# Expert biases moved from TensorE's matmuls to VectorE's additions, with merged tokens padded to 32 columns

## The chip, the cores and the metric

The kernel runs on one core of a Trainium2 chip. The metric is the device time of one execution in microseconds (us); of several executions the median is given. A core has five engines that work through their own queues: TensorE (matmuls and transposes, into PSUM), VectorE (DVE in the profile), ScalarE (ACT), GpSimd (POOL) and SyncE (SP), whose queue issues most of the DMAs. Everything here is computed in 32-bit floats, apart from a few small mask and bias operands in bf16.

## The reference, cut to what matters

Two transformer layers act on x of shape 8 x 512 x 256 (batch elements, tokens, channels). The first layer adds attention (16 heads of 64) and a mixture of 32 experts to x; the second adds a small associative memory and a feed-forward net with routed blocks. The change touches the experts of the first layer alone:

```python
logits = einsum('bsd,ed->bse', x, gate_w) + gate_b
probs = softmax(logits, axis=-2)                 # over the tokens
vals, idx = top_k(probs, 8)                      # each expert picks 8 tokens of each batch element
merged = einsum('bked,bke->bed', tok, vals)      # ... and merges them into one
h = einsum('bei,eih->beh', concat([merged, ones]), w1)   # 257 x 1024 an expert
h = gelu(h)
o = einsum('bej,ejo->beo', concat([h, ones]), w2)        # 1025 x 256 an expert
out = scatter-add of o * vals to the chosen tokens
```

So each expert sees eight merged tokens, one for each batch element. The last row of w1 (row 256) and of w2 (row 1024) of each expert is a bias: it is multiplied by one and added.

## The kernel before, in words

The program has three stretches. The first (to about 102 us) loads x, normalises it, transposes it, and computes the gate's logits, the chosen tokens' weights (`psel`) and the merged tokens. A merged token of expert e and batch element b is a column of `mT` (channels on the partitions; `mT` has an index for the channel half `dc`, the expert and the batch element, the last with 8 entries). The matmuls that merge (`pmg`, L373) are done for four batch elements at a time, and L380 copies the result to `mT`.

The second stretch (to about 1290 us) holds the attention, in 32 iterations (8 batch elements of 4 head groups), and the experts. Its order on TensorE, VectorE, ScalarE and GpSimd is written out by a planner (`Plan`, L49): each piece of work is an `op` with an engine, an estimated cost in ns, the pieces that it depends on, a priority in units of attention work, and the buffers (`acq`, `rel`) that it takes and gives back. The planner plays through time and always issues the piece that can start first within a horizon of 12 units. Each engine then works its list strictly in that order. SyncE's order is not among the planner's: the DMAs are put in a row when the program is built, by when what each waits for is expected. The buffers that matter here: `mm` and `tr` are two PSUM banks each, used by projections (`pq`, L456; `pv`, L464), by the output projection (`po`, L786) and by the experts' matmuls on the one hand, and by transposes (`pqk`, L514; `pgt`, L639; `pp`, L723), the attention's value matmuls (`y`, L756) and the experts' transposes on the other; `ew` are the six buffers for expert weights, 512 KB each.

The experts are worked in eight groups of four (`expert`, L845), one group for each batch element of attention, since the work of a group hides in that of the attention. Each of the four experts has a band of 32 PSUM partitions, of which the kernel before uses eight. A group has these steps:

1. Twice (once for each half of the 1024 hidden units): load four weight tiles, one an expert (L821). A bias matmul (L861) writes all 128 partitions of the bank with the experts' biases, from `b1g` (4 x 1024) and the selector `sel` as the stationary operand, and starts the accumulation. Then eight matmuls (L867), one for each expert and channel half, add their 8 x 512 products: the four experts' column bands of the array work side by side. VectorE copies the bank to `eh` (L874).
2. TensorE transposes `eh` (L888) in two sets of four into `tr` banks, and ScalarE applies Gelu from PSUM (L893), reading 8 of each 32 columns, into `ehT`. This gives the `tr` banks back.
3. Twice (once for each half of the hidden units): load four weight tiles (L828). In the first half a bias matmul (L918, from `b2g`) starts the accumulation. Sixteen matmuls (L925) follow. After the first half VectorE copies the bank to `osb` (L934). After the second it adds the bank to `osb` band by band, eight rows at a time (L938), and SyncE sends each band's rows to `o_all` (L940).

In the profile each 32-bit matmul stands as two matmul records, and a transposition as one: L867 has 256 records for its 128 instructions.

The third stretch (from about 1293 us) is the second layer. Its weights are first loaded into six tiles of the pool that held the expert weights (`raw1` twice, `raw2` twice, `raw3`, `raw4`; L980 to L983) and transposed (L1015, L1029, L1040 to L1051); then the batch elements follow each other.

Of the kernel before, what the change touches and what calls it, by code (L numbers as in the profile page):

```python
# [8 lines left out]
F32 = mybir.dt.float32  # L9
BF16 = mybir.dt.bfloat16  # L10
AF = mybir.ActivationFunctionType
ALU = mybir.AluOpType
# [127 lines left out]
def tile_two_layer_block(  # L140
# [31 lines left out]
    ewp = ctx.enter_context(tc.tile_pool(name="ew", bufs=6))  # L172
# [27 lines left out]
    for h in range(2):  # L200
# [22 lines left out]

    sel = const.tile([EPG, EPG, 32], F32, tag="sel", name="sel")
    nc.gpsimd.memset(sel, 0.0)
    nc.gpsimd.affine_select(
        out=sel, in_=sel, compare_op=ALU.not_equal, fill=1.0, base=0,
        pattern=[[-1, EPG], [0, 32]], channel_multiplier=1,
    )
# [62 lines left out]
    mT = const.tile([P, NC, E, B], F32, tag="mT", name="mT")  # L292
# [5 lines left out]
    with tc.tile_pool(name="pa", bufs=2) as pa, tc.tile_pool(name="pa1", bufs=1) as pa1:  # L298
# [86 lines left out]

        for h in range(2):
            nc.scalar.dma_start(w128[h * D : (h + 1) * D, 0:1], q_rms_w.unsqueeze(1))
            nc.scalar.dma_start(w128[h * D : (h + 1) * D, 1:2], k_rms_w.unsqueeze(1))
# [39 lines left out]
    with tc.tile_pool(name="pb", bufs=2) as pb, tc.tile_pool(name="pb1", bufs=1) as pb1:  # L428
# [5 lines left out]
            prT=2, yT=NPR * NHG + 3, xr=1, nm=3, sums=3, rinv=3, ew=6, eh=1, ehT=1, eb=1,  # L434
# [369 lines left out]
        def load_stage(m, w):  # L804
# [3 lines left out]
            def bias():  # L808
                rows = slice(g * EPG, (g + 1) * EPG)
                b1g = pb.tile([EPG, FH], F32, tag="b1g", name=f"b1g_{g}", bufs=1)  # L810
                nc.sync.dma_start(b1g, ew1[rows, C, :])
                b2g = pb.tile([EPG, C], F32, tag="b2g", name=f"b2g_{g}", bufs=1)
                nc.sync.dma_start(b2g, ew2[rows, FH, :])
                ebias[g] = b1g, b2g
# [30 lines left out]
        def expert(g, when):  # L845
# [7 lines left out]
            for half in range(2):  # L853
                ld = load_stage(4 * g + half, when[half] - NU)

                def hidden(half=half):
                    m = 4 * g + half
                    if half == 0:
                        s.h = pb.tile([P, FH], F32, tag="eh", name=f"eh_{g}", bufs=1)
                    s.ph = mm_tile(f"ph_{g}_{half}")  # L860
                    nc.tensor.matmul(  # L861
                        s.ph, sel.rearrange("k q r -> k (q r)"),
                        ebias[g][0][:, half * 512 : (half + 1) * 512], start=True, stop=False,
                    )
                    for dc in range(NC):
                        for q in range(EPG):
                            nc.tensor.matmul(  # L867
                                s.ph[32 * q : 32 * q + B, :], mT[:, dc, g * EPG + q, :],
                                ew[m, q][:, dc * 512 : (dc + 1) * 512],
                                start=False, stop=(dc == NC - 1),  # L870
                            )
# [4 lines left out]
                hd = op("PE", 2800, hidden, ld, when[half], acq=["mm"] + ["eh"] * (half == 0),  # L876
# [3 lines left out]
                def turn(half=half):  # L880
                    if half == 0:
                        s.hT = pb.tile(
                            [P, FH // P, EPG, B], F32, tag="ehT", name=f"ehT_{g}", bufs=1
                        )
# [14 lines left out]
                s.turn, s.gelu = turn, gelu  # L899
                out_ops.append((ho, turn, gelu))  # L900
            acts = []
            for half, (ho, turn, gelu) in enumerate(out_ops):
# [4 lines left out]
            for half, (ho, turn, gelu) in enumerate(out_ops):  # L907
                gl.append(op("ACT", 270 + 1283 * (1 - half), gelu, acts, when[2] + 0.1 + 0.01 * half,
                             rel=["tr"]))
            prev = []  # L910
            for half in range(2):
                ld = load_stage(4 * g + 2 + half, when[3 + half] - NU)

                def down(half=half):
                    m = 4 * g + 2 + half
                    s.po[half] = mm_tile(f"peo_{g}_{half}")
                    if half == 0:
                        nc.tensor.matmul(  # L918
                            s.po[0][:, :C], sel.rearrange("k q r -> k (q r)"), ebias[g][1],
                            start=True, stop=False,  # L920
                        )
                    for c in range(4):
                        for q in range(EPG):
                            k = half * 4 + c
                            nc.tensor.matmul(  # L925
                                s.po[half][32 * q : 32 * q + B, :C], s.hT[:, k, q, :],
                                ew[m, q][:, c * C : (c + 1) * C],
                                start=(half == 1 and c == 0), stop=(c == 3),
                            )

                def o_out(half=half):
                    if half == 0:
                        s.osb = pb.tile([P, C], F32, tag="osb", name=f"osb_{g}", bufs=1)
                        nc.vector.tensor_copy(s.osb, s.po[0][:, :C])  # L934
                        return
                    for q in range(EPG):
                        rows = slice(32 * q, 32 * q + B)
                        nc.vector.tensor_add(s.osb[rows, :], s.osb[rows, :], s.po[1][rows, :C])  # L938
# [310 lines left out]
```

## Time and profile before

| | us |
|---|---|
| Median of 3 runs | 1664.84 (1663.77 to 1667.19) |
| The profiled execution, its own time | 1665.2 |
| Span of the profiled execution | 1663.5 |
| TensorE busy | 1593.1 (96%) |
| VectorE busy | 922.3 (55%) |
| ScalarE busy | 700.5 (42%) |
| GpSimd busy | 590.7 (36%) |
| DMA, mean over the span | 54 GB/s |

A row of the profile names the source line, the engine, the operation, the tile written and the tile read, the shapes and the number of instructions. In rows of the timeline the first two numbers are the start and the length in us, and an entry in brackets is the time for which the engine stood idle before it and what released it. PE is TensorE at its matmuls, and PEld TensorE loading the stationary operand, which can overlap. For a matmul "128*8 128x512" means a stationary operand of 128 rows and 8 columns, and a moving one of 512 columns. Matmuls are pipelined, so the distance between the starts of two rows tells more than the length of one.

### The profile page before, as it was taken

The numbers are of one execution on the slowest core, as the hardware profiler recorded it, in microseconds if no ns is written. First come the engines' busy times: TensorE is split into PE (matmuls) and PEld (weight loads), VectorE is DVE, ScalarE is ACT, GpSimd is POOL, SyncE is SP. The second block draws the span as 40 slices with busy tenths as digits, with TensorE's granted clock in tenths as the row PEclk, the third lists the DMA queues.
The fourth block names the chain that finished last, engine by engine and source line by source line (L and its number), as shares of the span: only waits on it lengthen the run. The fifth ranks groups of instructions, "written<-read, shape, count | busy, mean of one in ns | idle before, by whom it ended". The sixth has DMA issues, their size and how long they took to land.

```text
span 1663.5 us, 26380 instructions
## 1 busy us (share of the span) xinstructions
PE 1593.1 (96%) x9416; PEld 933.3 (56%) x9416; DVE 922.3 (55%) x2682; ACT 700.5 (42%) x1918; POOL 590.7 (36%) x1082
## 2 busy tenths in 40 slices
PE   4789999999999999999999999999999899999999
PEld 1455555655665565565556556655655655555555
DVE  5537666666666665665666676666666332333331
ACT  1115554455446544544555454455545121222221
POOL 4016444444444444534444444444444100000000
PEclk9679999999999999999999999999999899999999
DMA  8000113032011302211130122123014000000000
GB/s 267 26 4 1 52 53 106 8 105 81 30 58 52 103 11 81 77 57 58 52 103 7 58 79 80 46 67 103 7 58 138 14 10 13 14 13 13 13 13 16
DMA packets 72914, 89.26 MB, mean 54 GB/s; under 512 B 5016, under 2 KB 55984, under 8 KB 72784
## 3 DMA queue, kind: packets, MB, share of 16 engines
q1 hardware_dynamic: 71552, 86.87, 16.0%
q8 instruction: 75, 1.23, 0.3%
q10 hardware_dynamic: 1232, 0.71, 0.2%
q14 instruction: 55, 0.45, 0.1%
HBM read 83.11 MB, written 4.19 MB: 52 GB/s over the span
## 4 chain that ended last, share of the span: by engine, by line
PE 89%; DVE 3%; ACT 1%; issue 1%; POOL 0%; ACTq 0%; DVEq 0%; POOLq 0%
PE pq L456 13%; PE sc L688 9%; PE pp L723 9%; PE y L756 9%; PE ph L1179 7%; PE py L1197 7%; PE po L786 7%; PE pv L464 6%; PE pqk L514 4%; PE sc L678 4%; PE peo L925 2%; PE ph L867 2%; PE sc L683 1%; PE ph L1183 1%; PE py L1195 1%; PE ph L861 1%
## 5 line engine op out<-in xcount | busy, mean ns | idle before, releaser
L710 POOL TENSOR_SCALAR pr<-pr,rinv 128x384 f32<-128x384 f32 (+3 forms) x512 | 265.9, 532 | 424.8 <-DVE rinv L707 244.3
L700 ACT ACTIVATE pr<-sc,nm 128x384 f32<-128x384 f32 (+3 forms) x512 | 266.2, 527 | 139.3 <-DVE nm L694 73.9
L241 POOL TENSOR_TENSOR rsqk<-ss,nhalf 128x8 f32<-128x8 f32 x128 | 210.8, 1647 | 146.5 <-DVE ss L491 140.9
L456 PE MATMUL pq<-wqk_sb,xnT 128*128 128x512 f32 x512 | 247.4, 606 | 3.3 <-DVE gl L482 3.3
L694 DVE TENSOR_REDUCE nm<-sc 128x2 f32<-128x768 f32 (+3 forms) x256 | 209.8, 823 | 73.4 <-PE sc L688 70.7
L723 PE MATMUL pp<-ident,pr 128*128 128x128 f32 x1280 | 218.9, 281 | 4.9 <-DVE prT L733 2.7
L723 PEld LDWEIGHTS pp<-ident,pr 128*128 128x128 f32 x1280 | 147.7, 141 | 122.0 <-issue 60.0
L688 PE MATMUL sc<-kT,qT 64*128 64x384 f32 (+3 forms) x1024 | 201.0, 471 | 0.0
L731 ACT COPY prT<-pp 128x384 f32<-128x384 f32 (+3 forms) x256 | 107.2, 426 | 156.4 <-PE pp L723 154.5
L733 DVE COPY prT<-pp 128x384 f32<-128x384 f32 (+3 forms) x256 | 123.4, 487 | 84.2 <-PE pp L723 81.2
L756 PE MATMUL y<-prT,v 128*64 128x256 f32 (+3 forms) x1024 | 152.2, 439 | 0.7 <-ACT prT L731 0.7
L464 PE MATMUL pv<-wvg_sb,xnT 128*128 128x260 f32 x512 | 136.4, 389 | 8.0 <-DVE osb L938 6.8
L456 PEld LDWEIGHTS pq<-wqk_sb,xnT 128*128 128x128 f32 x512 | 87.9, 192 | 85.3 <-issue 70.7
L1179 PE MATMUL ph<-xT,w1T 128*128 128x512 f32 x256 | 128.7, 620 | 0.0
L756 PEld LDWEIGHTS y<-prT,v 128*64 128x64 f32 x1024 | 68.4, 136 | 105.0 <-issue 63.4
L1197 PE MATMUL py<-w2T,hT 128*128 128x256 f32 x512 | 124.0, 388 | 0.0
L786 PE MATMUL po<-wp_sb,yT 128*128 128x256 f32 x512 | 116.4, 381 | 0.0
L1105 POOL TENSOR_TENSOR xres<-x,b_bc 128x1024 f32<-128x1024 f32 x8 | 18.8, 2344 | 265.1 <-DVE x L1098 265.1
L471 ACT ACTIVATE sq<-pq 128x512 f32<-128x512 f32 x128 | 76.3, 596 | 81.4 <-PE pq L456 78.6
L464 PEld LDWEIGHTS pv<-wvg_sb,xnT 128*128 128x128 f32 x512 | 89.0, 191 | 36.8 <-issue 14.6
L1197 PEld LDWEIGHTS py<-w2T,hT 128*128 128x128 f32 x512 | 93.3, 190 | 25.7 <-issue 15.3
L488 DVE TENSOR_REDUCE ss<-sq 128x8 f32<-128x512 f32 x128 | 87.4, 683 | 35.7 <-ACT sq L471 34.9
(187 smaller groups left out, 2067.7 us busy)
## 6 DMA issues: line engine op xcount, KB each, us to landing
ew<-in_L_ffn_w_dram SPq DMA_DIRECT2D x128, 512.0 KB
xt<-in_L_attn_x_dram SPq DMA_DIRECT2D x8, 512.0 KB
xr<-in_L_attn_x_dram SPq DMA_DIRECT2D x32, 128.0 KB
out_dram<-ot SPq DMA_DIRECT2D x32, 128.0 KB
raw<-in_L_ffn_w_dram SPq DMA_DIRECT2D x4, 512.0 KB
wqk_sb<-in_L_attn_Wq_dram SPq DMA_DIRECT2D x2, 512.0 KB
wqk_sb<-in_L_attn_Wk_dram SPq DMA_DIRECT2D x2, 512.0 KB
wvg_sb<-in_L_attn_Wv_dram SPq DMA_DIRECT2D x2, 512.0 KB
```

The source lines that it names most:

```text
L241: nc.gpsimd.tensor_tensor(r, src, nhalf[:, :n], ALU.pow)
L456: nc.tensor.matmul(s.pq[t], xnT[b][:, dc, cols], wqk_sb[:, dc, g, :], start=(dc == 0), stop=(dc == NC - 1),)
L464: nc.tensor.matmul(s.pv[t][:, : GW + HG], xnT[b][:, dc, cols], wvg_sb[:, dc, g, :], start=(dc == 0), stop=(dc == NC - 1),)
L688: nc.tensor.matmul(m.sc[:, h, :w], s.qT[k, q, n0:w], s.kT[k, q, :w], start=False, stop=True)
L694: nc.vector.tensor_reduce(m.nm, m.sc[:, :, :w], AX.X, ALU.max, negate=True)
L700: nc.scalar.activation(m.p[:, h, :], m.sc[:, h, :w], AF.Exp, bias=m.nm[:, h : h + 1], accum_out=m.sums[:, h : h + 1],)
L710: nc.gpsimd.tensor_scalar(m.p[:, h, :], m.p[:, h, :], m.rinv[:, h : h + 1], 1.0, ALU.mult, ALU.mult)
L723: nc.tensor.transpose(m.pt[h][:, d * P : (d + 1) * P], m.p[:, h, j * P : (j + 1) * P], ident)
L756: nc.tensor.matmul(pp.yp[h * D : (h + 1) * D, j * P :], s.v[j][:, hh * D : (hh + 1) * D], pp.tri[:, h, j : j + 4 * (NT - 1 - j) + 1 : 4, : ...
L786: nc.tensor.matmul(o.po[:, :C], yT[b * nk + k][:, t * P : (t + 1) * P], wp_sb[:, k, :], start=(k == 0), stop=(k == nk - 1),)
L1179: nc.tensor.matmul(ph, w1T[:, dc, k * P : (k + 1) * P], s.xT[:, dc, :], start=(dc == 0), stop=False,)
L1197: nc.tensor.matmul(py[:, :C], hT[:, c, cols], w2T[:, c, :], start=False, stop=(c == NFC - 1),)
```

## The change

The bias matmuls are left out. The hidden layer's bias is loaded once in the first stretch (`eb1`, 32 x 1024), transposed by eight small transposes and kept as `eb1T`; VectorE adds it, broadcast over the 32 columns of each expert, when it moves the transposed hidden units from PSUM to `ehT`. Gelu then runs on ScalarE from `ehT` to itself, and the `tr` bank is given back by VectorE's addition. The output's bias is loaded to all 32 partitions of each band by four broadcast DMAs per group, and VectorE adds it where it copied the first half's bank. As no matmul fills the other 24 rows of a band any more, the merged tokens are padded: `mT` gets 32 columns for each expert, cleared once by GpSimd, and the experts' matmuls write all 32 rows of their band. The second half's bank is added by one instruction over 128 rows instead of four over 8. To make room in SBUF the weight buffers go from six to five. The planner's costs are set anew; each expert matmul step is now given 1716 ns.

```diff
-    ewp = ctx.enter_context(tc.tile_pool(name="ew", bufs=6))
+    ewp = ctx.enter_context(tc.tile_pool(name="ew", bufs=5))
...
-    sel = const.tile([EPG, EPG, 32], F32, tag="sel", name="sel")
-    nc.gpsimd.memset(sel, 0.0)
-    nc.gpsimd.affine_select(
...
-    mT = const.tile([P, NC, E, B], F32, tag="mT", name="mT")
+    eb1T = const.tile([P, FH // P, E], F32, tag="eb1T", name="eb1T")
+    mT = const.tile([P, NC, E, 32], F32, tag="mT", name="mT")
+    nc.gpsimd.memset(mT, 0.0)
...
+        eb1 = pa1.tile([E, FH], F32, tag="eb1", name="eb1")
+        nc.sync.dma_start(eb1, ew1[:, C, :])
+        pb1T = tr_tile("pb1T")
+        for k in range(FH // P):
+            nc.tensor.transpose(
+                pb1T[:, k * E : (k + 1) * E], eb1[:, k * P : (k + 1) * P], ident[:E, :E]
+            )
+        nc.vector.tensor_copy(eb1T, pb1T[:, : FH // P * E].rearrange("p (k e) -> p k e", e=E))
...
-            prT=2, yT=NPR * NHG + 3, xr=1, nm=3, sums=3, rinv=3, ew=6, eh=1, ehT=1, eb=1,
+            prT=2, yT=NPR * NHG + 3, xr=1, nm=3, sums=3, rinv=3, ew=5, eh=1, ehT=1, eb=1,
...
-                b1g = pb.tile([EPG, FH], F32, tag="b1g", name=f"b1g_{g}", bufs=1)
-                nc.sync.dma_start(b1g, ew1[rows, C, :])
-                b2g = pb.tile([EPG, C], F32, tag="b2g", name=f"b2g_{g}", bufs=1)
-                nc.sync.dma_start(b2g, ew2[rows, FH, :])
-                ebias[g] = b1g, b2g
+                ebias[g] = pb.tile([P, C], F32, tag="b2g", name=f"b2g_{g}", bufs=1)
+                for q in range(EPG):
+                    nc.sync.dma_start(
+                        ebias[g][32 * q : 32 * (q + 1), :],
+                        ew2[g * EPG + q, FH, :].partition_broadcast(32),
+                    )
...
-                    nc.tensor.matmul(
-                        s.ph, sel.rearrange("k q r -> k (q r)"),
-                        ebias[g][0][:, half * 512 : (half + 1) * 512], start=True, stop=False,
-                    )
                     for dc in range(NC):
                         for q in range(EPG):
                             nc.tensor.matmul(
-                                s.ph[32 * q : 32 * q + B, :], mT[:, dc, g * EPG + q, :],
+                                s.ph[32 * q : 32 * (q + 1), :], mT[:, dc, g * EPG + q, :],
                                 ew[m, q][:, dc * 512 : (dc + 1) * 512],
-                                start=False, stop=(dc == NC - 1),
+                                start=(dc == 0), stop=(dc == NC - 1),
                             )
...
-                hd = op("PE", 2800, hidden, ld, when[half], acq=["mm"] + ["eh"] * (half == 0),
+                hd = op("PE", 1716, hidden, ld, when[half], acq=["mm"] + ["eh"] * (half == 0),
...
-                            [P, FH // P, EPG, B], F32, tag="ehT", name=f"ehT_{g}", bufs=1
+                            [P, FH // P, EPG, 32], F32, tag="ehT", name=f"ehT_{g}", bufs=1
...
                 def gelu(half=half):
-                    nc.scalar.activation(
-                        s.hT[:, half * 4 : (half + 1) * 4],
-                        s.pt[half].rearrange("p (c q r) -> p c q r", c=4, q=EPG)[:, :, :, :B],
-                        AF.Gelu,
-                    )
+                    hT = s.hT[:, half * 4 : (half + 1) * 4]
+                    nc.scalar.activation(hT, hT, AF.Gelu)
+
+                def bias(half=half):
+                    c = slice(half * 4, (half + 1) * 4)
+                    nc.vector.tensor_add(
+                        s.hT[:, c],
+                        s.pt[half].rearrange("p (c q r) -> p c q r", c=4, q=EPG),
+                        eb1T[:, c, g * EPG : (g + 1) * EPG].unsqueeze(3).to_broadcast(
+                            [P, 4, EPG, 32]
+                        ),
+                    )
...
-                acts.append(tn)
+                acts.append(op("DVE", 598, bias, [tn], when[2] + 0.05 + 0.01 * half, rel=["tr"]))
...
-                gl.append(op("ACT", 270 + 1283 * (1 - half), gelu, acts, when[2] + 0.1 + 0.01 * half,
-                             rel=["tr"]))
+                gl.append(op("ACT", 586 + 1283 * (1 - half), gelu, acts, when[2] + 0.1 + 0.01 * half))
...
-                    if half == 0:
-                        nc.tensor.matmul(
-                            s.po[0][:, :C], sel.rearrange("k q r -> k (q r)"), ebias[g][1],
-                            start=True, stop=False,
-                        )
...
-                        nc.vector.tensor_copy(s.osb, s.po[0][:, :C])
+                        nc.vector.tensor_add(s.osb, s.po[0][:, :C], ebias[g])
                         return
+                    nc.vector.tensor_add(s.osb, s.osb, s.po[1][:, :C])
                     for q in range(EPG):
-                        rows = slice(32 * q, 32 * q + B)
-                        nc.vector.tensor_add(s.osb[rows, :], s.osb[rows, :], s.po[1][rows, :C])
...
-                dn = op("PE", 1750 + 350 * (half == 0), down, ld + gl, when[3 + half], acq=["mm"],
+                dn = op("PE", 1716, down, ld + gl, when[3 + half], acq=["mm"],
...
-                prev = [op("DVE", 334 if half == 0 else 1350, o_out, [dn] + prev,
+                prev = [op("DVE", 334, o_out, [dn] + prev,
```

More of the change, by code (lines that the diff above doesn't have):

```diff
@@ L222, in tile_two_layer_block @@
                 )
-    sel = const.tile([EPG, EPG, 32], F32, tag="sel", name="sel")
-    nc.gpsimd.memset(sel, 0.0)
-    nc.gpsimd.affine_select(
-        out=sel, in_=sel, compare_op=ALU.not_equal, fill=1.0, base=0,
-        pattern=[[-1, EPG], [0, 32]], channel_multiplier=1,
-    )
     nhalf = const.tile([P, 64], F32, tag="nhalf", name="nhalf")
@@ L808, in bias @@
             def bias():
-                rows = slice(g * EPG, (g + 1) * EPG)
-                b1g = pb.tile([EPG, FH], F32, tag="b1g", name=f"b1g_{g}", bufs=1)
-                nc.sync.dma_start(b1g, ew1[rows, C, :])
-                b2g = pb.tile([EPG, C], F32, tag="b2g", name=f"b2g_{g}", bufs=1)
-                nc.sync.dma_start(b2g, ew2[rows, FH, :])
-                ebias[g] = b1g, b2g
+                ebias[g] = pb.tile([P, C], F32, tag="b2g", name=f"b2g_{g}", bufs=1)
[4 more added lines that the diff above has]
+                    )
             def weights(q):
@@ L892, in gelu @@
                 def gelu(half=half):
-                    nc.scalar.activation(
-                        s.hT[:, half * 4 : (half + 1) * 4],
-                        s.pt[half].rearrange("p (c q r) -> p c q r", c=4, q=EPG)[:, :, :, :B],
-                        AF.Gelu,
-                    )
-                s.turn, s.gelu = turn, gelu
-                out_ops.append((ho, turn, gelu))
+                    hT = s.hT[:, half * 4 : (half + 1) * 4]
[8 more added lines that the diff above has]
+                        ),
+                    )
+                out_ops.append((ho, turn, bias, gelu))
             acts = []
-            for half, (ho, turn, gelu) in enumerate(out_ops):
+            for half, (ho, turn, bias, gelu) in enumerate(out_ops):
                 tn = op("PE", 436, turn, [out_ops[0][0], out_ops[1][0]], when[2] + 0.01 * half,
                         acq=["tr"] + ["ehT"] * (half == 0), rel=["eh"] * (half == 1))
-                acts.append(tn)
+                acts.append(op("DVE", 598, bias, [tn], when[2] + 0.05 + 0.01 * half, rel=["tr"]))
             gl = []
-            for half, (ho, turn, gelu) in enumerate(out_ops):
-                gl.append(op("ACT", 270 + 1283 * (1 - half), gelu, acts, when[2] + 0.1 + 0.01 * half,
-                             rel=["tr"]))
+            for half, (ho, turn, bias, gelu) in enumerate(out_ops):
+                gl.append(op("ACT", 586 + 1283 * (1 - half), gelu, acts, when[2] + 0.1 + 0.01 * half))
             prev = []
@@ L925, in down @@
                             nc.tensor.matmul(
-                                s.po[half][32 * q : 32 * q + B, :C], s.hT[:, k, q, :],
+                                s.po[half][32 * q : 32 * (q + 1), :C], s.hT[:, k, q, :],
                                 ew[m, q][:, c * C : (c + 1) * C],
-                                start=(half == 1 and c == 0), stop=(c == 3),
+                                start=(c == 0), stop=(c == 3),
                             )
```

## The prediction

> **What bounds the kernel now.** I read the totals by engine and the chain that ended last, then the busy time of each engine by stretch, then TensorE's own rows around the four places that the change touches, then its waits.
>
> The page's totals, and the head of its chain:
>
> ```profile
> PE 1593.1 (96%) x9416; PEld 933.3 (56%) x9416; DVE 922.3 (55%) x2682; ACT 700.5 (42%) x1918; POOL 590.7 (36%) x1082
> ...
> PE 89%; DVE 3%; ACT 1%; issue 1%; POOL 0%; ACTq 0%; DVEq 0%; POOLq 0%
> ```
>
> Busy time by stretch (length, then PE, PEld, DVE, ACT, POOL, granted clock, DMA share, GB/s); the rows of one batch element in mid-run:
>
> ```profile
> 325.00:473.00 148.00, 146.71 (x995) 86.78 (x992) 95.58 (x272) 76.40 (x224) 67.29 (x124) 1.00 0.19 62
> 473.00:621.00 148.00, 145.99 (x980) 86.23 (x979) 94.55 (x266) 75.64 (x223) 67.28 (x124) 1.00 0.19 62
> ```
>
> TensorE is busy 146 of 148 us at the full granted clock; VectorE has a third of its time free, ScalarE half, DMA four fifths. What leaves TensorE's queue there leaves the time, unless another engine then makes it wait.
>
> **Part 1: 24 bias matmuls go.** TensorE's rows around a hidden-layer step and an output step:
>
> ```profile
> 176.95 0.44 PE L723 MATMUL pp<-ident,pr 128*128 128x128 f32 x2
> 177.32 1.12 PE L861 MATMUL ph<-b1g,sel 4*128 4x512 f32 x2
> 178.37 1.90 PE L867 MATMUL ph<-ew,mT 128*8 128x512 f32 x16
> 180.21 0.44 PE L723 MATMUL pp<-ident,pr 128*128 128x128 f32 x2
> ```
>
> ```profile
> 246.13 0.69 PE L918 MATMUL peo<-b2g,sel 4*128 4x256 f32 x2
> 246.76 1.91 PE L925 MATMUL peo<-ew,ehT 128*8 128x256 f32 x32
> 248.60 0.44 PE L723 MATMUL pp<-ident,pr 128*128 128x128 f32 x2
> ```
>
> From start to start L861 holds the queue 178.37 - 177.32 = 1.05 us and L918 0.62 us; the records give 1.051 in all 16 cases and 0.624 in all 8. The change of array tiling that L867 and L925 pay (0.20 us from the row before) is paid today by the bias matmul, and the second L925 of a group, which has no bias ahead of it, pays the same 0.20; so the whole 1.05 and 0.62 go. 16 x 1.051 + 8 x 0.624 = **-21.8 us**.
>
> **Part 2: the stationary operand grows from 8 to 32 columns.** No row has 32. Weight loads (PEld) of the first rounds, of L867 with 8 columns and of L756 with 64:
>
> ```profile
> 178.37 0.12 PEld L867 LDWEIGHTS ph<-ew,mT 128*8 128x8 f32 x8 [0.76 <-issue]
> 178.81 0.11 PEld L867 LDWEIGHTS ph<-ew,mT 128*8 128x8 f32 x4 [0.32 <-issue]
> ...
> 250.75 0.20 PEld L756 LDWEIGHTS y<-prT,v 128*64 128x64 f32 x4 [0.76 <-ACT qT L519]
> 251.23 0.14 PEld L756 LDWEIGHTS y<-prT,v 128*64 128x64 f32 x2 [0.28 <-issue]
> ```
>
> The first round takes 0.44 us with 8 columns and 0.48 with 64; the later rounds of 512 columns take 0.43 in both. So 24 more columns cost some 0.02 us once in each of 32 steps: +0.6 us (0 to 1.5, the latter at 64 columns' price). The Trainium skill speaks against this: "TensorE: Matmul & The Clock Gate" says under "LDWEIGHTS" that a load takes columns / 1.2 ns, so 20 ns more each, and under "Measured speedup vs the span model" that a load overlaps a running matmul only when the row group differs. The four experts' tiles share all rows, so by the page 768 loads would cost +15.4 us in the open. The records show the second round's loads starting 2 ns after a matmul of the same rows has begun (178.802 after 178.800), so they do overlap here; I take **+0.6**, and keep 15.4 only as an outer end. With it the sum below would be -10.
>
> **Part 3: the output addition of a group.** After the second output step TensorE stands still for a PSUM buffer, which VectorE frees only after four additions of 8 rows. VectorE's row, TensorE's (each: start, length), then the wait in total (us, times, longest):
>
> ```profile
> 258.76 1.76 DVE L938 TENSOR_TENSOR osb<-osb,peo 8x256 f32<-8x256 f32 x4 [0.73 <-PE peo L925]
> ```
>
> ```profile
> 260.58 1.15 PE L464 MATMUL pv<-wvg_sb,xnT 128*128 128x260 f32 x4 [0.97 <-DVE osb L938]
> ```
>
> ```profile
> PE pv L464 <- DVE osb L938: 6.8, 7, 1.0
> ```
>
> One addition over 128 rows costs what L794 of the same operands does, 0.424 us. The buffer is then free at 259.2, before TensorE would ask for it (about 259.6): **-6.8 us**. VectorE gains 8 x (1.76 - 0.42) = 10.7. The first half's copy (L934, 0.425) becomes an addition at the same price.
>
> **Part 4: the new addition between transposes and Gelu.** 16 VectorE instructions 128x512 from PSUM with a broadcast operand; L498 is that form, 0.69 us: 11 us, which cancels the 10.7. In VectorE's total (95 of 148) it is covered. Its latency is not all covered. The addition now frees the transposes' PSUM buffers, of which there are two, and the queues of the built program show the two sets of transposes back to back in seven groups of eight, where they had other work between them in the kernel before (in all but the last group 1.9 us of L456 or 0.9 of L464). In four of those seven the gate's transposes (L639) and then a pp transposition follow at once, in the last group two pp; all need these buffers. By the rows (transposes 0.11 us apart, 0.27 for the last one's end, 0.69 for an addition): the first addition ends some 1.4 us after the first transposition starts and TensorE is there at 0.87, so it waits 0.5; the next buffer comes 0.69 later, TensorE is back after 0.22, so 0.45 more. 5 x 0.95 = **+4.8 us** (0 to 10: none if VectorE runs ahead, double if it is behind when the transposes end). Behind the waiting addition in VectorE's queue stand gT, prT and tm, for which the next score and transposition steps wait; that is the upper end. In two groups an L456 follows, whose 1.9 us cover the addition.
>
> Gelu reads 128x512 instead of 128x128: 0.60 (L471's price at that size) for 0.275, +5.2 us on ScalarE, covered by its idle half; table loads stay 34.
>
> **Part 5: the new order.** The planner's costs change, so the interleaving does. Counted in the built queues, TensorE changes tiling 637 times instead of 652 between the first projection and the last; a transposition is followed 0.109 us later by one of its kind and 0.205 later by L678: 15 x 0.095 = **-1.4 us**. TensorE's other waits in that phase stay as they are (some 2.5 us per batch element, from what start-to-start times exceed their usual value).
>
> **Part 6: five weight buffers for six.** The tightest place lies between a group's two output steps: of the second step's four loads, two now wait for the first step to end; with five buffers three will. Today:
>
> ```profile
> 248.68 1.38 SPq L828 DMA_DIRECT2D ew<-in_L_ffn_w_dram  x2
> ```
>
> ```profile
> 256.70 1.91 PE L925 MATMUL peo<-ew,ehT 128*8 128x256 f32 x32
> ```
>
> The two land at 252.7 and 254.2, 2.5 us before 256.70; each further load in a row lands about 1 us later, so a third lands some 7.3 us after the release. In the new queue the second step comes later: the work between them, at the durations of before, is 10.5 to 12.2 us (8.2 before) and 8.8 in the last group. **0**. The four bias loads per group (SP queue, 0.45 us each, ahead of loads needed 60 us later) and the xr loads behind a weight load keep their places: 0. At the end the second layer's last staging tile (raw4, three small loads) must now wait for the transposes of raw1: issued at about 1308.4 instead of 1285.3, landed by 1312 (2.3 us as xr), needed at 1313.0: 0 (up to +2).
>
> **Part 7: the start.** Clearing mT is one 128x2048 POOL memset; 128x512 took 0.51, so 2.0 us, while sel's two go (0.5) and slope, phalf and gtm (1.2) move behind the first reciprocal roots: the first root is done by about 14.0, and VectorE is busy until 15.1. The eb1 load (0.5 us of SP) precedes two x loads, a weight load (1.4) moves behind them. Eight small transposes (0.11 each) stand where TensorE waits 0.78 us for pselT. 0, within -1 and +1.5.
>
> **Sum.** -21.8 + 0.6 - 6.8 + 4.8 - 1.4 = **-24.6 us**. The profiled execution took 1665.2 (span 1663.5, 1.7 around it): 1640.6. The median of the runs is 0.4 lower: **1640**.
>
> **Rivals.**
> A. The gain is larger: VectorE is ahead when the transposes end, and earlier freed transposition buffers also take away the waits that follow them today (L723 for prT 2.7 us, L678 for pr 1.5). -29.4 to -34: 1630 to 1635. For it: Gelu held these buffers through a 1.28 us table load. Against: the back-to-back transposes.
> B. The gain is smaller: the additions stall TensorE by their upper end (10), and the output's wait returns for another late engine once TensorE runs ahead (half of 6.8): -21.8 + 0.6 - 3.4 + 10 - 1.4 = -16: 1649, and with the ends of parts 2, 6 and 7 (1 to 2 us each) 1652. For it: TensorE is the only engine that gets shorter.
> C. Slower: the third weight load is late in every group. Each microsecond past TensorE's arrival is 8 us in all; it eats the 24.6 when a load lands 3.1 us past a gap of about 12, some 15 us after the release; at 16 us the time would be 1672. Today's landings, 4, 5, 6 and 7 us after issue for four in a row, speak against it.
> That the change doesn't do what it says is excluded by the built queues: no matmul of L861 or L918 is left.
>
> **How the numbers follow.** 1640 with 54% (1635 to 1646 its own range), A 21%, B 20%, C 3% slower, 2% within 0.2% (3.3 us, about what a measurement of this kernel can tell from no change). The range 1630 to 1652 takes in A down to 1630 and B to 1652. Faster 95%, same 2%, slower 3%.
>
> **What would show it.** No bias matmuls; L867 and L925 steps still 1.83 and 1.84 us from first start to the next row, within 0.05; no wait of L464 for osb; waits of L639 and L723 for ehT's addition of 3 to 7 us in all; no wait of L925 or L867 for DMA; a batch element in about 145 us instead of 148.5. Wrong if the steps of L867 and L925 lengthen by 0.3 us or more (weight loads in the open), or if a row of TensorE names a weight load as what it waited for.

## The result, and the profile after

The changed kernel takes **1643.7 us** (median of four runs, 1642.5 to 1645.0), the kernel before beside it 1664.9 (1663.8 to 1667.2). The ratio is 0.9871, with a 95% interval of 0.9857 to 0.9885: 21 us faster, where 24.6 were forecast and 1640 named. A second comparison gave 1645.5 against 1666.1, ratio 0.9878 (0.9862 to 0.9894).

The totals by engine, and the head of the chain that ended last, of the changed kernel:

```profile
PE 1574.0 (96%) x9376; PEld 931.4 (57%) x9376; DVE 918.1 (56%) x2675; ACT 699.8 (43%) x1918; POOL 591.2 (36%) x1081
...
PE 86%; DVE 3%; POOL 2%; ACT 2%; issue 1%; DMA 0%; ACTq 0%; POOLq 0%; DVEq 0%
```

TensorE's busy time fell by 19.1 us and the span by 20.4, so its idle time shrank by only 1.3 us, though 6.8 us of waiting for `osb` were to go. Its share of the chain fell from 89% to 86%, and POOL (0 before) and ACT took some of it: new waits have appeared.

Busy time by stretch, two batch elements in mid-run (length, then PE, PEld, DVE, ACT, POOL, granted clock, DMA share, GB/s):

```profile
325.00:473.00 148.00, 146.78 (x1007) 87.19 (x999) 95.91 (x274) 77.84 (x228) 68.58 (x126) 1.00 0.19 63
473.00:621.00 148.00, 147.27 (x1004) 89.30 (x1003) 96.22 (x273) 77.84 (x229) 67.65 (x126) 1.00 0.22 69
```

TensorE works through more in the same window (1007 and 1004 instructions for 995 and 980) and is as full as before; VectorE is busy 0.3 and 1.7 us longer in them, ScalarE 1.4 and 2.2 us.

Where the time went is told by TensorE's starts. The first projection starts at 102.05 us (101.95 before) and the output projections that close the attention at 1273.18 (1293.36 before); what follows is as long as it was. So the whole gain lies in the second stretch.

TensorE's rows at a hidden-layer step and at the weight loads under it, and then at the two output steps of a group (start, length, engine, line):

```profile
177.06 0.44 PE L728 MATMUL pp<-ident,pr 128*128 128x128 f32 x2
177.43 0.16 PEld L868 LDWEIGHTS ph<-ew,mT 128*32 128x32 f32 x8 [0.17 <-issue]
177.43 1.92 PE L868 MATMUL ph<-ew,mT 128*32 128x512 f32 x16
177.88 0.13 PEld L868 LDWEIGHTS ph<-ew,mT 128*32 128x32 f32 x4 [0.30 <-issue]
...
179.28 0.44 PE L728 MATMUL pp<-ident,pr 128*128 128x128 f32 x2
```

```profile
243.68 1.93 PE L927 MATMUL peo<-ew,ehT 128*32 128x256 f32 x32
245.54 0.44 PE L728 MATMUL pp<-ident,pr 128*128 128x128 f32 x2
...
258.59 1.88 PE L461 MATMUL pq<-wqk_sb,xnT 128*128 128x512 f32 x4
258.79 0.37 ACT L736 COPY prT<-pp 128x256 f32<-128x256 f32 x1 [2.34 <-PE pp L728]
258.91 0.41 DVE L938 TENSOR_TENSOR osb<-osb,peo 128x256 f32<-128x256 f32 x1
```

The hidden step holds TensorE from 177.43 to 179.28, and no bias matmul stands ahead of it; an output step holds it 1.86 us. The addition of the output is one instruction of 0.41 us where four took 1.76, and TensorE is at its next projection, not waiting.

TensorE's waits in the second stretch (total in us, times, longest):

```profile
PE pq L461 <- DVE gl L487: 3.7, 11, 0.7
PE sc L683 <- ACT pr L705: 2.0, 4, 1.4
PE pv L469 <- DVE tm L503: 1.4, 4, 0.6
PE pgt L644 <- DVE ehT L900: 1.4, 4, 0.3
PE pp L728 <- POOL pr L715: 1.3, 2, 0.8
PE pp L728 <- POOL xr L627: 1.2, 7, 0.2
PE pe L889 <- ACT prT L736: 1.0, 1, 1.0
PE pp L728 <- DVE ehT L900: 0.9, 4, 0.2
```

The wait for `osb` (6.8 us before) is gone. The two for `ehT` are those forecast for the new addition. The rest was forecast to stay as it was, and did not: in the same stretch before, the same wait of `pq` for `gl` was 2.0 us, and no single wait but those for `osb` was longer than 0.7.

This list leaves out what is shorter than it can see. A finer account takes the distance from each of TensorE's starts to the next, between the first projection and the last output projection, and compares it with what the same pair of rows takes when nothing is late (the 10th percentile of such pairs over all kernels here): the sum of these is the work, what is above is waiting. "Ramp" is the first 75 us, "last group" everything from 8 us before the transposes of the last expert group on. Between the three columns and the length remain 13 to 15 us of small scatter. The length is read off the trace. How the rest divides into work and waits is an estimate: with other ways to form the pairs single entries move by some us.

| kernel | length of the stretch, us | work | waits: ramp | mid-run | last group |
|---|---|---|---|---|---|
| before | 1205.1 | 1132.8 | 13.8 | 37.4 | 7.1 |
| after | 1184.8 | 1109.6 | 13.8 | 34.8 | 12.9 |
| after, second profile | 1182.5 | 1109.6 | 12.7 | 34.7 | 12.1 |
| one_add | 1197.5 | 1132.8 | 13.8 | 29.1 | 7.1 |
| no_bias | 1174.7 | 1111.0 | 12.7 | 29.2 | 7.0 |
| narrow | 1184.5 | 1109.6 | 13.8 | 34.8 | 12.6 |
| after_six | 1186.0 | 1111.3 | 13.8 | 36.3 | 11.4 |
| old_order_wide | 1188.3 | 1111.0 | 13.8 | 40.4 | 8.2 |
| old_order_narrow | 1179.5 | 1111.0 | 13.8 | 32.4 | 7.5 |
| after_oldcosts | 1175.1 | 1112.2 | 12.7 | 27.9 | 7.4 |
| cost_hidden | 1177.2 | 1111.9 | 13.5 | 29.4 | 7.4 |
| cost_true | 1175.9 | 1111.8 | 12.6 | 29.6 | 6.8 |
| oldcosts_narrow | 1175.0 | 1112.2 | 13.8 | 26.7 | 7.3 |
| apart | 1189.5 | 1111.1 | 13.8 | 39.4 | 11.8 |

The work fell by 23.2 us, as forecast (21.8 and 1.4; the 20 ns more of each expert step fall into the scatter); as the forecast and this column are both made of row-to-row distances, the agreement is no test of its own. Of the 4.3 us that the stretch fell short of the forecast, nearly all is in the last group: waits there went from 7.1 to 12.9 where about 8 were expected. A count that needs no pairs says the same. Between the last hidden-layer step and the closing projections the same 304 records of TensorE stand in every kernel here without bias matmuls; they take 37.2 us in no_bias, 37.8 in after_oldcosts, and 42.3 and 41.1 in the two profiles of the changed kernel.

### The profile page after: what moved, and what is told of

The parts are those of the page before. It is cut to its first block, busy times and chain, and to the rows that moved or that the text cites. A ratio compares the mean times of both kernels' runs of the same rounds, so it can differ in the third digit from the quotient of the medians.

```text
span 1643.1 us, 26263 instructions
## 1 busy us (share of the span) xinstructions
PE 1574.0 (96%) x9376; PEld 931.4 (57%) x9376; DVE 918.1 (56%) x2675; ACT 699.8 (43%) x1918; POOL 591.2 (36%) x1081
## 4 chain that ended last, share of the span: by engine, by line
PE 86%; DVE 3%; POOL 2%; ACT 2%; issue 1%; DMA 0%; ACTq 0%; POOLq 0%; DVEq 0%
PE pq L461 12%; PE sc L693 9%; PE pp L728 9%; PE y L761 9%; PE ph L1180 7%; PE py L1198 7%; PE po L791 7%; PE pv L469 6%; PE sc L683 3%; PE pqk L519 3%; PE ph L868 2%; PE peo L927 2%; PE ph L1184 1%; PE py L1196 1%; PE sc L688 1%; POOL pr L715 1%
## 5 line engine op out<-in xcount | busy, mean ns | idle before, releaser
L234 POOL TENSOR_TENSOR rsqk<-ss,nhalf 128x8 f32<-128x8 f32 x128 | 210.7, 1646 | 192.3 <-DVE ss L496 187.2
L503 DVE TENSOR_TENSOR tm<-pq,rsqk 128x512 f32<-128x512 f32 x128 | 88.2, 689 | 39.2 <-POOL rsqk L234 37.8
```

The costliest lines, as they stand in the source:

```text
L234: nc.gpsimd.tensor_tensor(r, src, nhalf[:, :n], ALU.pow)
```

## The experiments

The first four compare with the kernel before at 1666.7 us (1664.2 to 1667.9), the next four at 1666.1 (1661.9 to 1667.5), the next three at 1665.9 (1661.5 to 1667.6) and the last at 1666.9 (1665.7 to 1668.1).

**one_add: the wide output addition alone.** The kernel before, bias matmuls and all, but the experts' matmuls read 32 columns (8 of their own and the next 24 in memory), so that the second half's bank can be added by one instruction.

```diff
...
+                    nc.vector.tensor_add(s.osb, s.osb, s.po[1][:, :C])
                     for q in range(EPG):
-                        rows = slice(32 * q, 32 * q + B)
-                        nc.vector.tensor_add(s.osb[rows, :], s.osb[rows, :], s.po[1][rows, :C])
```

> The kernel before with one change: the experts' outputs fill all 32 rows of a band (the stationary operand reads 32 columns, 24 of them belonging to the next experts, whose rows nobody uses), so that the second half is added by one instruction over 128 rows instead of four over 8. Bias matmuls, six weight buffers, the planner's costs and TensorE's order stay. Theory (the wait of pv for osb is pure loss on the path): -6.8 for the wait and +0.6 for loading 32 columns instead of 8, together -6.2 us against the kernel before, some 1658.7. Rival (the wait turns up elsewhere, since TensorE then only runs ahead of VectorE): +0.6 to -1 us, 1664 to 1665.5.

Measured: 1660.2 us, ratio 0.9954 (0.9942 to 0.9967), a gain of 6.5 by the medians; the stretch is 7.6 us shorter, all in mid-run waits. The wait for `osb` was pure loss, and no other wait takes its place.

**no_bias: the bias matmuls taken away.** one_add without its 24 bias matmuls and with nothing in their place: both biases of the experts are left out of the computation.

```diff
-                    nc.tensor.matmul(
-                        s.ph, sel.rearrange("k q r -> k (q r)"),
-                        ebias[g][0][:, half * 512 : (half + 1) * 512], start=True, stop=False,
-                    )
...
-                    if half == 0:
-                        nc.tensor.matmul(
-                            s.po[0][:, :C], sel.rearrange("k q r -> k (q r)"), ebias[g][1],
-                            start=True, stop=False,
-                        )
```

> The same as one_add, and the 24 bias matmuls are left out, with nothing in their place: the experts' biases are missing from the result. The order of all other TensorE work stays. Theory (TensorE's time is the time): -21.8 more, in all -28.0 us against the kernel before, some 1637. Rival (with TensorE shorter other engines' chains become the bound): less than 15 us of the 21.8 come through, 1644 or more.

Measured: 1635.3 us, ratio 0.982 (0.9803 to 0.9838); 24.9 us below one_add by the medians; the stretch is 22.8 us shorter. What leaves TensorE leaves the time. But here lies the first surprise: the changed kernel has no more work on TensorE than this one, and its stretch is 10.1 us longer (7.8 in its second profile); by the medians it takes 8.4 us more. The complete change gives back eight to ten microseconds somewhere.

**narrow: a quarter of the new VectorE and ScalarE work.** The changed kernel with the addition and Gelu on the 8 real columns of each 32.

```diff
-                        s.pt[half].rearrange("p (c q r) -> p c q r", c=4, q=EPG),
+                        s.pt[half].rearrange("p (c q r) -> p c q r", c=4, q=EPG)[:, :, :, :B],
...
-                            [P, 4, EPG, 32]
+                            [P, 4, EPG, B]
```

> The changed kernel with one thing different: the addition of the hidden bias and Gelu work on the 8 columns of each expert that are used instead of all 32 (128x128 instead of 128x512, so some 0.27 us instead of 0.69 for the addition and 0.28 instead of 0.63 for Gelu); the experts' stationary operands still read 32 columns, which overlap. TensorE's order, the buffers and the planner's costs stay. Theory (the length of the addition is what TensorE waits for after the back-to-back transposes): four groups lose waits of 0.51 and 0.38, two 0.25, the last some 0.6 and part of its Gelu, together -4 to -6 us against the changed kernel, 1638 to 1640. Rival (the waits come from the order, not from the addition's length): 0, 1643 to 1644.

Measured: 1646.1 us, ratio 0.9876 (0.9862 to 0.9889), nothing gained on the changed kernel's 0.9871: the theory falls. The waits for `ehT` are gone from the list:

```profile
PE pq L463 <- DVE gl L489: 4.4, 12, 0.7
PE y L763 <- ACT prT L738: 3.1, 4, 0.8
PE sc L685 <- ACT pr L707: 2.0, 4, 1.4
```

In their place `y` waits 3.1 us for a copy of ScalarE (0.8 in the changed kernel). The total in mid-run is the same 34.8. In this order a wait that is removed comes back some 7 us later, under another name. The trace shows what holds it there. The changed kernel, then narrow, whose stretch starts 1.2 us later:

```profile
369.30 0.69 DVE L503 TENSOR_TENSOR tm<-pq,rsqk 128x512 f32<-128x512 f32 x1
374.63 2.38 PE L761 MATMUL y<-prT,v 128*64 128x512 f32 x16 [0.20 <-ACT prT L736]
```

```profile
370.48 0.69 DVE L505 TENSOR_TENSOR tm<-pq,rsqk 128x512 f32<-128x512 f32 x1 [0.59 <-POOL rsqk L234]
375.82 2.37 PE L763 MATMUL y<-prT,v 128*64 128x512 f32 x16 [0.78 <-ACT prT L738]
```

The shorter additions set VectorE free 0.6 us earlier, but `tm` also needs `rsqk`, which GpSimd works on for 1.65 us and which ends at the same moment of the stretch in both kernels. VectorE waits there for 0.59 us, what follows on VectorE and ScalarE (`nm`, the exponentials, `prT`) is no earlier, and `y` starts where it did. So it is in all four groups.

**after_six: six weight buffers again.** The changed kernel with six buffers in the pool and in the planner (`mT` overlapping to make room).

```diff
-    ewp = ctx.enter_context(tc.tile_pool(name="ew", bufs=5))
+    ewp = ctx.enter_context(tc.tile_pool(name="ew", bufs=6))
```

> The changed kernel with six weight buffers again, in the pool and in the planner (room is made by letting the 32 columns of mT overlap). Theory (with five buffers no load is late): within 2 us of the changed kernel, 1642 to 1646, what differs being the planner's order. Rival (the missing 3 to 4 us of the forecast went into later weight loads): 1640 or less.

Measured: 1646.9 us, ratio 0.9889 (0.9874 to 0.9904), 0.9 us above the theory's range and far from the rival's 1640. The order differs too (655 changes of tiling for 637). The buffers are not where the eight to ten microseconds are.

**old_order_wide and old_order_narrow: the additions in the order of before.** TensorE's instructions stand exactly as in no_bias; VectorE's addition is issued just ahead of Gelu, inside the same piece of the planner's work, which has no cost of its own for it. The second is the same with 128 columns for 512.

```diff
+                    nc.vector.tensor_add(
+                        s.hT[:, c],
+                        s.pt[half].rearrange("p (c q r) -> p c q r", c=4, q=EPG),
+                        eb1T[:, c, g * EPG : (g + 1) * EPG].unsqueeze(3).to_broadcast(
+                            [P, 4, EPG, 32]
+                        ),
...
+                    nc.scalar.activation(s.hT[:, c], s.hT[:, c], AF.Gelu)
```

> The whole change, but TensorE's instructions keep the order that they have in the kernel before (the bias matmuls just fall out of it), with six weight buffers and the planner's costs of before; the hidden bias is added by VectorE (128x512) in front of Gelu in the same place of ScalarE's work. Theory 'the new order of the planner costs the missing 4 us and more': TensorE's matmuls are those of no_bias, which took 1635.3, so 1635 to 1638, ratio 0.981 to 0.983, and the stretch from the first pq to the last po 1174.7 to 1177. Rival 'the additions themselves, in whatever order, hold TensorE up': the four stalls of about 1 us and the 5.9 us of the last group return, 1641 to 1646, ratio 0.985 to 0.988.

> As old_order_wide, but the addition and Gelu work on the 8 real rows of each 32 (128x128 instead of 128x512). If the addition's length is hidden in the old order (theory), the same time as old_order_wide within 1.5 us. If the additions themselves are what TensorE waits for (rival), 3 to 6 us less than old_order_wide.

Measured: 1650.2 us, ratio 0.9903 (0.9889 to 0.9917), and 1640.9 us, ratio 0.985 (0.9836 to 0.9864). Both theories fall here: in an order made without them, the additions cost 0.8% and 0.3% over no_bias, more than the rival allowed (1646), and their length counts (9.3 us, where the rival had 3 to 6). TensorE's longest waits of old_order_wide, and then who waited for its addition:

```profile
PE pp L734 <- DVE rinv L718: 5.9, 4, 1.5
PE sc L689 <- ACT pr L711: 5.1, 4, 1.6
```

```profile
L902 DVE TENSOR_TENSOR ehT<-pe,eb1T x16: 671/680/685, 223.8 to 1249.2; 128x512 f32<-128x512 f32 x16
...
  ACT ehT L909: 5.8, 8
  PE pp L734: 0.7, 1
```

TensorE hardly waits for the addition itself. ScalarE does: Gelu stands in its queue where it could start at once from PSUM, and now it waits there for VectorE, 0.7 us in each of eight groups, and then takes 0.63 us where it took 0.275. The softmax's exponentials behind it (`pr`) are late, with them the reciprocals (`rinv`), and TensorE waits for those: 5.1 and 5.9 us against 1.5 and 1.3 in the kernel before. That the waiting Gelu makes them late is read from the queues; no run moves it alone.

**after_oldcosts: the planner's costs of before.** The changed kernel, five buffers and wide additions included, with three cost estimates put back.

```diff
-                hd = op("PE", 1716, hidden, ld, when[half], acq=["mm"] + ["eh"] * (half == 0),
+                hd = op("PE", 2800, hidden, ld, when[half], acq=["mm"] + ["eh"] * (half == 0),
...
-                dn = op("PE", 1716, down, ld + gl, when[3 + half], acq=["mm"],
+                dn = op("PE", 1750 + 350 * (half == 0), down, ld + gl, when[3 + half], acq=["mm"],
...
-                prev = [op("DVE", 334, o_out, [dn] + prev,
+                prev = [op("DVE", 334 if half == 0 else 1350, o_out, [dn] + prev,
```

> The changed kernel with three planner costs put back to those of before (hidden step 2800, output step 2100 and 1750, output addition 1350), nothing else: in its queue other work stands between the two sets of hidden transposes again. Theory (order): 3 to 7 us below the changed kernel, 1637 to 1641, ratio 0.982 to 0.9855. Rival (the additions, or the five buffers with them): as the changed kernel, ratio 0.987, within 1.5 us.

Measured: **1636.9 us**, ratio 0.9827 (0.9813 to 0.9842), 8.6 us less than the changed kernel beside it. Every engine has the same number of instructions as in the changed kernel; their order differs. By the table work rises by 2.6 us (665 changes of tiling for 637), waits fall by 6.9 in mid-run and 5.5 in the last group. The same place in both kernels, first the changed one, then this one:

```profile
365.01 1.04 PE L469 MATMUL pv<-wvg_sb,xnT 128*128 128x260 f32 x4
365.89 1.06 PE L889 MATMUL pe<-ident,eh 128*128 128x128 f32 x8
367.29 0.38 PE L644 MATMUL pgt<-ident,gtm 128*128 128x128 bf16 x4 [0.34 <-DVE ehT L900]
367.89 0.66 PE L728 MATMUL pp<-ident,pr 128*128 128x128 f32 x4 [0.22 <-DVE ehT L900]
```

```profile
364.84 0.61 PE L889 MATMUL pe<-ident,eh 128*128 128x128 f32 x4
365.28 1.04 PE L469 MATMUL pv<-wvg_sb,xnT 128*128 128x260 f32 x4
366.16 0.60 PE L889 MATMUL pe<-ident,eh 128*128 128x128 f32 x4
366.60 0.60 PE L728 MATMUL pp<-ident,pr 128*128 128x128 f32 x4
```

With a projection between the two sets of transposes, as in all groups but the last, the first addition is done when the next PSUM buffer is wanted, and no instruction of any engine waits for L900 any more.

TensorE's waits after the last group's hidden layer, in the changed kernel (1235 to 1275 us) and in after_oldcosts (1225 to 1266 us):

```profile
PE sc L683 <- ACT pr L705: 1.4, 1, 1.4
PE pp L728 <- POOL pr L715: 1.3, 2, 0.8
PE pe L889 <- ACT prT L736: 1.0, 1, 1.0
PE sc L683 <- DVE gT L651: 0.5, 1, 0.5
PE pp L728 <- DVE prT L738: 0.5, 1, 0.5
PE pp L728 <- DVE rinv L712: 0.4, 1, 0.4
```

```profile
PE pp L728 <- ACT prT L736: 1.5, 3, 0.6
PE sc L683 <- ACT pr L705: 1.0, 1, 1.0
PE pgt L644 <- ACT prT L736: 0.5, 1, 0.5
```

**after_again: the changed kernel beside it.** No edit.

> The changed kernel itself, for a comparison on the same chip: ratio 0.987 as measured before. If the 3.9 us wait of one y step in the last batch element goes with a half granted clock that comes only in some executions, it is missing in this profile or comes in another place; if it comes from the order of the work, it stands in the same place, about 1269 us.

Measured: 1645.5 us, ratio 0.9878 (0.9862 to 0.9894). Its waits behind the last group are the six lines above to the tenth, so they belong to the order of the work. What differed is the granted clock: in 1268.5 to 1272.0 us it was 0.51 in the first profile and 1.00 in this one; the last group's waits differ by 0.8 us between the two.

**cost_hidden and cost_true: which cost, and what value.** The changed kernel with the hidden step's cost alone put back; and with both of TensorE's step costs set to what the trace shows.

```diff
-                hd = op("PE", 1716, hidden, ld, when[half], acq=["mm"] + ["eh"] * (half == 0),
+                hd = op("PE", 2800, hidden, ld, when[half], acq=["mm"] + ["eh"] * (half == 0),
```

```diff
-                hd = op("PE", 1716, hidden, ld, when[half], acq=["mm"] + ["eh"] * (half == 0),
+                hd = op("PE", 1860, hidden, ld, when[half], acq=["mm"] + ["eh"] * (half == 0),
...
-                dn = op("PE", 1716, down, ld + gl, when[3 + half], acq=["mm"],
+                dn = op("PE", 1870, down, ld + gl, when[3 + half], acq=["mm"],
```

> The changed kernel with one planner cost put back, that of the hidden-layer step (2800 for 1716). The two sets of hidden transposes stand apart again in TensorE's queue, as with all three costs put back. Theory 'what costs the changed kernel its 8.6 us is that TensorE is told of a hidden step 1.1 us shorter, which pulls the two sets of transposes together and the work after them with it': the time of after_oldcosts, 1636 to 1639, ratio 0.982 to 0.9845. Rival 'the output costs set the waits of the last batch element, 5 to 6 us': 1641 to 1643, ratio 0.985 to 0.9865, with waits of 12 to 13 us from the last group's hidden steps on.

> The changed kernel with the two step costs of TensorE set to what the trace shows (hidden 1860, output 1870 for 1716). In its queue three groups of eight have the two sets of transposes back to back, against seven in the changed kernel and none with 2800. If the back-to-back transposes and what follows them make the loss in proportion (theory): between, 1639 to 1643, ratio 0.984 to 0.986. If a truer cost is enough (rival): 1636 to 1638, ratio 0.982 to 0.983.

Measured: 1638.4 us, ratio 0.9829 (0.9816 to 0.9843), and 1636.4 us, ratio 0.9818 (0.9805 to 0.9832). One number, the hidden step's estimate, is enough for the gain, and the rival of cost_true was right: two estimates that are 8% too short (1716 for 1854 to 1867 ns) separate its order from the bad one. The forecast "in proportion to the back-to-back transposes" fell. Of cost_true's three such groups two are followed by a projection that covers the addition, which leaves one uncovered against five; that is a reading after the fact, and the last experiment tests it.

**oldcosts_narrow: the best order with the short addition.** after_oldcosts and narrow together; TensorE's order is that of after_oldcosts.

> after_oldcosts (the changed kernel with the three planner costs of before) with the addition and Gelu on the 8 real rows of each 32 (128x128 for 128x512); TensorE's instructions stand in the very order of after_oldcosts. Theory: in this order nothing waits for the addition, so within 1.5 us of after_oldcosts, ratio 0.982 to 0.984. Rival: VectorE's and ScalarE's shorter work takes away some of the 28.5 us of waits left, as it did between old_order_wide and old_order_narrow: 1630 to 1634, ratio 0.979 to 0.981.

Measured: **1634.9 us**, ratio 0.981 (0.9797 to 0.9824). The time lies between the two forecasts, and the interval overlaps that of after_oldcosts (0.9827); the stretch is the same to 0.2 us, as the theory says. A complete version that beats both kernels: 31 us under the one, about 11 under the other.

**apart: only the two sets of transposes moved apart.** The changed kernel with its own costs and a later due time for the second set.

```diff
-                tn = op("PE", 436, turn, [out_ops[0][0], out_ops[1][0]], when[2] + 0.01 * half,
+                tn = op("PE", 436, turn, [out_ops[0][0], out_ops[1][0]], when[2] + 0.5 * half,
...
-                acts.append(op("DVE", 598, bias, [tn], when[2] + 0.05 + 0.01 * half, rel=["tr"]))
+                acts.append(op("DVE", 598, bias, [tn], when[2] + 0.05 + 0.5 * half, rel=["tr"]))
```

> The changed kernel with the second set of hidden transposes due half a unit later than the first (0.5 for 0.01), the planner's costs as the change has them. Transpositions of the probabilities now stand between the two sets in the six groups of mid-run; in the last group they stay back to back and the order after them is that of the changed kernel. Theory 'the waits of mid-run come from the transposes that stand together': those waits fall from 35 to 28 to 31 us and the 12 to 13 us of the last group stay, so 1638 to 1641.5, ratio 0.983 to 0.985. Rival 'the waits move along the queue whatever stands between the transposes, as in narrow': mid-run stays at 34 to 36 us, 1643 to 1646, ratio 0.986 to 0.988.

Measured: 1649.0 us, ratio 0.9888 (0.9871 to 0.9906), outside both forecasts on the slow side. Eight transpositions of `pp`, with `pgt` or a projection in their middle, now stand between the sets in the six groups of mid-run, and the waits there rose from 34.8 to 39.4:

```profile
PE sc L683 <- ACT pr L705: 6.1, 4, 2.4
PE pq L461 <- DVE gl L487: 2.6, 7, 0.7
...
PE pgt L644 <- DVE ehT L900: 1.4, 4, 0.3
```

`pgt` still waits 1.4 us for the addition and the scores wait longer for ScalarE. So the loss is not in the two sets being neighbours as such. But the test is weaker than it was meant to be. `pp` takes a `tr` bank as the second set did, so `pgt` stands before the same wait; the projection that stands there in after_oldcosts takes none. And Gelu waits for both additions: its table load starts 3.3 us after the first set here (373.08 after 369.78) and 0.8 us after it in the changed kernel (366.71 after 365.89).

## Why the prediction was right, and which step was not

**Parts 1 and 2, the matmuls: right.** From one_add to no_bias the stretch went down by 22.8 us where 21.8 were forecast. The hidden steps take 1.854 to 1.857 us to the next row for 1.834 to 1.836, the output steps 1.864 to 1.867 for 1.844 to 1.845: 20 ns for each of 32 steps, 0.64 us for the 0.6 forecast. By the Trainium skill's page "TensorE: Matmul & The Clock Gate" the estimate was 15.4 us, from its figure under "LDWEIGHTS" and its rule that a load overlaps a running matmul only where the row group differs (it stands there under "The mechanism"); the measurement decides against it, for these column-tiled matmuls. The first round of loads takes 0.45 us (177.43 to 177.88), between the 0.44 read at 8 columns and the 0.48 at 64.

**Part 3, the output addition: right.** one_add alone gained 6.5 us, and 7.6 in the stretch, for 6.8 (6.2 with the wider weight loads that it has too).

**Part 4, the hidden addition: right in size and place, not in what it means.** Start to start, TensorE loses 0.51 us to the first and 0.38 to the second of the instructions behind the transposes in the four groups named (0.5 and 0.45 forecast), and 0.6 in the last: 4.2 us for 4.8. (In the two groups that a projection covers it loses 0.25, but as much in narrow, so that is not the addition's length.) The list of waits has 2.3 us, a little under the 3 to 7 that the prediction asked for. But narrow took these waits away and gained nothing. The step treated them as a loss that stands by itself; narrow shows that a chain through GpSimd's `rsqk` holds the same instructions until the same moment. Gelu's 0.63 us from SBUF (0.60 forecast) stayed hidden in the changed order, and did not in old_order_wide, where ScalarE had to wait for VectorE.

**Part 5, the order: the step that failed.** Its 1.4 us for 15 fewer changes of tiling stands in the work column too (1111.0 in no_bias, 1109.6), but no run isolates it. Its other sentence, that TensorE's other waits stay as they are, is wrong. In the last group they went from 7.1 to 12.9 us (12.1 in the second profile) where Part 4 allowed one more; that is about the 4 us between 1640 and 1643.7. In mid-run the sum came out near (34.8, from 37.4 - 6.8 + 3.8 = 34.4), but a better order has 28, so the agreement there is in part luck: Parts 4 and 5 together put the changed kernel 3.4 us above a kernel without any bias work, and its stretch is 10.1 us above that of no_bias (7.8 in the second profile). The forecast time is near because the 28 us of Parts 1 to 3, which are right, make up most of it. Putting back the estimate of the hidden step alone, with every instruction of the change in place, gives 7.1 us, all three 8.6: gains of 27.5 and 29.2 us on the kernel before, where 24.6 were forecast. What is shown: the loss hangs on the order that the estimate of 1716 ns leads to, not, in that order, on the additions' length. The three orders made with 1716 (the changed kernel, after_six with its six buffers, apart) took 1643.7 to 1649.0 us, the three with 1860 or 2800 (cost_true, cost_hidden, after_oldcosts) 1636.4 to 1638.4. Which of the moved instructions cause the late exponentials and probabilities stays open; laid side by side the two queues of TensorE differ in hundreds of places, and the one cut through them (apart) missed.

**Parts 6 and 7: right.** No wait of TensorE for the experts' weights is in the trace, six buffers gained nothing, the last stretch is as long as before and the first 0.1 us longer. A batch element takes 145.2 us on average from one group's transposes to the next's, for 148.5 before; 145 was forecast.

Of the rivals, A (waits vanish and more is gained) did not come with this order; the planner's old costs bring the change near its range (1636.9 for 1630 to 1635). B (the additions at their upper end, and the output's wait returning elsewhere) had the right sense that waits move, at a size that old_order_wide shows (1650.2). C did not come.

## What to carry to other kernels

When an edit also changes what a scheduler is told, cost the order as a change of its own: run the new instructions under the old estimates, as here, and the old instructions under the new ones, which was not done here. A wait on the list is worth its length only if what stands behind it is not late as well, and the way to know is to shorten its cause alone: with `osb` it was worth all, with `ehT` nothing. Look at the last round of a pipeline by itself; here most of what was lost against the forecast lay there (42.3 us for 37.2).

## What the runs showed of the hardware

Twenty-four more columns of the stationary operand cost 20 ns once in a step of 16 or 32 matmul records, not per load: from the second round on, each weight load of such a step starts 2 ns after a matmul on the same 128 rows has begun (177.882 after 177.880 in the changed kernel) and runs beside it. A Gelu of 128x512 from SBUF took 0.63 us, of 128x128 from PSUM 0.275. After a stretch with several idle gaps the granted TensorE clock was 0.51 over 1268.5 to 1272.0 us in one execution and 1.00 in another of the same kernel, in which those gaps stand to the tenth:

```profile
1268.50:1272.00 3.50, 3.50 (x11) 1.87 (x12) 0.42 (x1) 0.37 (x1) 0.21 (x1) 0.51 0.48 164
```

```profile
1268.50:1272.00 3.50, 3.50 (x20) 2.32 (x21) 0.00 (x0) 0.85 (x2) 0.00 (x0) 1.00 0.33 107
```

(Window, length, then busy PE, PEld, DVE, ACT, POOL, the granted clock, DMA share and GB/s; first profile, then second.)
